# A recurrent layer and a gated feed-forward layer on one core: h transposed by VectorE and transfers instead of TensorE

## The chip, the core and the metric

The kernel runs on one core of a Trainium2 chip. A core has TensorE (PE in the profile; its weight loads are PEld), VectorE (DVE), ScalarE (ACT), GpSimd (POOL) and SyncE (SP), which here issues the data transfers. Each engine runs its own instructions in the order in which they were written, and waits on semaphores where it needs another's result. The metric is the device time of one execution in microseconds. Before the change the median of three runs is 543.51 us (543.43 to 544.18).

## What is computed

Two layers in a row, each with a layer norm before it and one behind it, and a residual sum. x is (2, 1024, 512), all in float32. Cut to what matters:

```python
def rnn(x, W_in, b_in, W_out, b_out, gamma, beta):        # hidden 1024
    u = einsum('bsd,hd->bsh', x, W_in) + b_in
    s_t = tanh(u_t + s_{t-1} * gamma + beta)              # 1024 steps in time
    return einsum('bsh,dh->bsd', s, W_out) + b_out

def ffn(x, gate_w, up_w, down_w, gate_scale, up_scale, down_scale):   # inner 1536
    q(x, w, scale) = (x @ w.astype(float8_e4m3fn).astype(float32)) * scale
    return q(silu(q(x, gate_w, gate_scale)) * q(x, up_w, up_scale), down_w, down_scale)

x = x + layernorm(rnn(layernorm(x), ...))
x = x + layernorm(ffn(layernorm(x), ...))
```

## The kernel before

The 1024 time steps of each of the two sequences are cut into 8 segments that run side by side, so a step works on 16 columns (2 sequences x 8 segments) of 1024 hidden values, a tile of 128x128. A segment is 128 steps, taken in 8 blocks of 16 steps; a block holds 16 x 16 = 256 tokens, which is two token tiles of 128 (numbers i = 2k and 2k + 1 of block k). The segments start from states that are warmed up over 96 steps first. All of it is one program, and the order of the work on every engine is written out by hand.

The first part (to about 168 us of the profile) loads and rounds the weights, computes u for all blocks, and runs the warm-up and the steps of blocks 0 and 1. The part that the change touches is the loop from L545 on. It goes over 8 blocks k of 12 slices fc, and one slice is one column of 128 of the inner 1536. In slice i:

- TensorE: `mm_g(i)` multiplies the gate and up weights with h of block k, 16 matmuls of 256 columns, h being given as two parts hT and hL (a rounded value and what the rounding left), then `down(i - 2)` adds two earlier results, each as the parts fH and fL, into the two token tiles of the block, 4 matmuls of 512 columns. `mm_g` uses three buffers in turn.
- ScalarE: `gate(i - 1)`, the Silu, then the rounded part fH.
- VectorE: `f_in(i - 1)` (f, L447), and `f_low(i - 1)` (fL, L455), which `down(i - 1)` needs in slice i + 1. Both come one slice behind `mm_g`.

Between these, the loop carries three other strands, in slices chosen by hand:

1. `main_step(k + 2, t)`, the recurrence of the block after the next: two instructions on VectorE (z, L260 and L261), a tanh on ScalarE (L262), each step waiting for the one before. `STEPS` says how many of a block's 16 steps stand in each slice: the first of the pair is for steps ahead of `f_low`, the second for steps behind it. `go(n)` writes up to n of them; `go(K)` all that are left of the slice. Blocks 6 and 7 have none.
2. What makes h of block k + 1, for its two token tiles: `mm_y` (output projection, 8 products of 512 columns in two passes each, L384), `y_in` (bias and statistics, L394 and L116), `y_resid` (residual sum onto the rows of x, and statistics, L401), `y_norm` (h, L409), `trans_h` (four transposes on TensorE into PSUM, L130) and `split_h` (hT by ScalarE, L423, hL by VectorE, L424). Statistics go on to GpSimd (`var`, `rstd`), which gives the reciprocal deviation; the row behind it on VectorE waits for that. The rows of x are loaded again by `load_r` (L376) at the end of slice 1, as their buffers (four in turn) come free: a load waits until `o_out` of block k - 1 has read the buffer. In block 0 there are no `mm_y` and no loads in the loop: the first four token tiles are projected and loaded ahead of it, and the first two (block 0's own) go through `trans_h` and `split_h` there.
3. What ends block k - 1: `o_in`, `o_stat`, `o_out` in slice 1, and two stores of 256 KB on SyncE ahead of the two loads. `check_piece` (L493, ScalarE, slices 3, 6, 9 and 11 of blocks 0 to 5) and `verdict` (slice 7 of block 6) check that the segmented result may be used; a fallback program follows that is not run here.

Before the change the slices of strand 2 are: `mm_y` in 1 and 4, `y_in` in 2 and 5, `y_resid` in 4 and 6, `y_norm` in 4 and 8, `trans_h` in 5 and 9, `split_h` in 6 and 10.

`us[0]` is the tile of block 0's states (8 KB of each partition); after the first two `mm_y`, and the first step of block 1, nothing reads it.

Of the kernel before, what the change touches and what calls it, by code (L numbers as in the profile page):

```python
# [9 lines left out]
F32 = mybir.dt.float32  # L10
# [4 lines left out]
ALU = mybir.AluOpType  # L15
# [3 lines left out]
P = 128  # L19
# [13 lines left out]
def segmented(  # L33
# [21 lines left out]
    nc = tc.nc  # L55
# [3 lines left out]
    ND, NH, NI = D // P, H // P, I // P  # L59
# [54 lines left out]
    def stats(src):  # L114
        st = small.tile([P, nc.vector.BN_STATS_DIM], F32, tag="st", name="st")
        nc.vector.bn_stats(st, src)  # L116
        return mean_rstd(st)
# [10 lines left out]
    def transposed(pt, src):  # L128
        for dc in range(ND):
            nc.tensor.transpose(pt[:, dc, :], src[:, dc * P : (dc + 1) * P], ident)  # L130

    us = {}
# [12 lines left out]
    held = {}  # L145
# [112 lines left out]
    def main_step(k, t):  # L258
        z = small.tile([P, NH, GB], F32, tag="z", name=f"z_{k}_{t}", bufs=2)
        nc.vector.tensor_tensor(z, coef, run["state"], ALU.mult)  # L260
        nc.vector.tensor_tensor(z, z, us[k][:, :, t], ALU.add)  # L261
        nc.scalar.activation(us[k][:, :, t], z, AF.Tanh)  # L262
        run["state"] = us[k][:, :, t]
# [67 lines left out]
    for n in range(NB - 1):  # L331
        mine = []
        for t in range(K):
# [26 lines left out]
            if n in (1, 2, 3, 4) and t == 9:  # L360
                c = slice((n - 1) * NH // 4, n * NH // 4)
# [17 lines left out]
    def mm_y(i, part=range(NH)):  # L379
        k, t0 = i // 2, (i % 2) * TT  # L380
        if part[0] == 0:
            held["py", i] = ps_y.tile([P, D], F32, tag="py", name=f"py_{i}")
        for hc in part:
            nc.tensor.matmul(  # L384
                held["py", i],
                lhsT=us[k][:, hc, t0 : t0 + TT, :].rearrange("p t q -> p (t q)"),
                rhs=wout_sb[:, hc, :],
                start=(hc == 0),
                stop=(hc == NH - 1),
            )  # L390

    def y_in(i):
        y = held["y", i] = yw.tile([P, D], F32, tag="y", name=f"y_{i}", bufs=1)
        nc.vector.tensor_tensor(y, held["py", i], bout_bc, ALU.add)  # L394
        held["ymr", i] = stats(y)

    def y_resid(i):

        m, r = held["ymr", i]
        x1 = held["x", i]  # L400
        nc.vector.scalar_tensor_tensor(x1, held["y", i], r, x1, ALU.mult, ALU.add)  # L401
        c = held["c", i] = small.tile([P, 1], F32, tag="c", name=f"c_{i}", bufs=8)
        nc.gpsimd.tensor_tensor(c, m, r, ALU.mult)
        held["xmr", i] = stats(x1)

    def y_norm(i):
        m, r = held["xmr", i]
        h = held["h", i] = yw.tile([P, D], F32, tag="h", name=f"h_{i}")
        nc.vector.tensor_scalar(h, held["x", i], m, r, ALU.subtract, ALU.mult)  # L409

    def trans_h(i):
        pool, tag = (ps_d, "pd") if i == 1 else (ps_t, "pt")
        pt = held["ph", i] = pool.tile([P, ND, P], F32, tag=tag, name=f"ph_{i}")
        transposed(pt, held["h", i])

    def split_h(i):

        k, j = i // 2, i % 2
        if j == 0:
            held["hT", k] = hw.tile([P, ND, N], F32R, tag="hT", name=f"hT_{k}")  # L420
            held["hL", k] = hw.tile([P, ND, N], F32R, tag="hL", name=f"hL_{k}")
        hT, hL = (held[a, k][:, :, j * P : (j + 1) * P] for a in ("hT", "hL"))
        nc.scalar.copy(hT, held["ph", i])  # L423
        nc.vector.tensor_tensor(hL, held["ph", i], hT.bitcast(F32), ALU.subtract)  # L424


    def mm_g(i):
        k, fc = divmod(i, NI)
        pg = held["g", i] = ps_g.tile([P, 2, N], F32, tag="pg", name=f"pg_{i}")
        for n, w in enumerate((gate_sb, up_sb)):  # L430
            for dc in range(ND):
                for part in ("hT", "hL"):
                    nc.tensor.matmul(  # L433
                        pg[:, n, :],
                        lhsT=w[:, dc, fc * P : (fc + 1) * P],
                        rhs=held[part, k][:, dc, :],
                        start=(dc == 0 and part == "hT"),
                        stop=(dc == ND - 1 and part == "hL"),
                    )

    def gate(i):
        g = held["gate", i] = fw.tile([P, N], F32, tag="gate", name=f"gate_{i}")
        nc.scalar.activation(g, held["g", i][:, 0, :], AF.Silu, scale=ffs[:, 0, i % NI : i % NI + 1])  # L443

    def f_in(i):
        f = held["f", i] = fw.tile([P, N], F32, tag="f", name=f"f_{i}")
        nc.vector.scalar_tensor_tensor(  # L447
            f, held["g", i][:, 1, :], ffs[:, 1, i % NI : i % NI + 1], held["gate", i], ALU.mult, ALU.mult
        )
        fH = held["fH", i] = fw.tile([P, N], F32R, tag="fH", name=f"fH_{i}")  # L450
        nc.scalar.copy(fH, f)  # L451

    def f_low(i):
        fL = held["fL", i] = fw.tile([P, N], F32R, tag="fL", name=f"fL_{i}")
        nc.vector.tensor_tensor(fL, held["f", i], held["fH", i].bitcast(F32), ALU.subtract)  # L455

    def down(i, j):
        k, fc = divmod(i, NI)
        if fc == 0:
            held["d", 2 * k + j] = ps_d.tile([P, D], F32, tag="pd", name=f"pd_{k}_{j}")  # L460
        for part in ("fH", "fL"):
            nc.tensor.matmul(  # L462
                held["d", 2 * k + j],
                lhsT=held[part, i][:, j * P : (j + 1) * P],
                rhs=down_sb[:, fc, :],
                start=(fc == 0 and part == "fH"),
                stop=(fc == NI - 1 and part == "fL"),
            )

    def o_in(i):  # L470
        o = held["o", i] = pool.tile([P, D], F32, tag="o", name=f"o_{i}", bufs=2)
        nc.vector.tensor_tensor(o, held["d", i], dsc_bc, ALU.mult)
# [49 lines left out]
    n = NB - 1  # L522
# [17 lines left out]
    mm_y(3, range(6, NH))  # L540


    STEPS = {0: (1, 0), 1: (1, 3), 3: (1, 1), 4: (0, 3), 7: (1, 0), 8: (0, 1), 9: (1, 0), 10: (0, 1), 11: (1, 1)}
    last = NB * NI - 1
    for i in range(last + 3):  # L545
        k, fc = divmod(i, NI)
        more = k + 1 < NB
        steps = iter(())
        if k + 2 < NB:
            t0 = sum(sum(STEPS.get(c, ())) for c in range(fc))  # L550
            before, after = STEPS.get(fc, (0, 0))
            steps = iter(range(t0, t0 + before + after))

        def go(n):
            for t in islice(steps, n):
                main_step(k + 2, t)

        if i <= last:
            mm_g(i)
        if i >= 2:  # L560
            for j in range(2):
                down(i - 2, j)
        if more:
            if fc == 1 and k:
                mm_y(2 * k + 2)
            if fc == 4 and k:
                mm_y(2 * k + 3)
            if fc in (5, 9):
                trans_h(2 * k + 2 + (fc - 5) // 4)
        live = 1 <= i <= last + 1  # L570
        if live:
            gate(i - 1)
            f_in(i - 1)

        if more and fc == 2:
            y_in(2 * k + 2)
        elif more and fc == 4:
            y_resid(2 * k + 2)
        elif more and fc == 5:
            y_in(2 * k + 3)  # L580
        elif more and fc in (6, 10):
            split_h(2 * k + 2 + (fc - 6) // 4)
        elif more and fc == 8:
            y_norm(2 * k + 3)
        else:
            go(1)
        if live:
            f_low(i - 1)
        ends = [2 * k - 2, 2 * k - 1] if k else []
        if fc == 1 and k:  # L590
            for j in ends:
                o_in(j)
            go(1)
        if k and fc == (1 if more or k == NB else 2):
            for j in ends:
                o_stat(j)
            go(1)
        for j in ends:
            if fc == (1 if more or k == NB else 3 + j % 2):
                o_out(j)  # L600
                go(1)
        if more and fc == 1 and k:
            for j in range(2):
                load_r(2 * k + 2 + j)
        if more and fc == 4:
            go(2)
            y_norm(2 * k + 2)
        if more and fc == 6:
            y_resid(2 * k + 3)
        go(K)  # L610
        if k + 2 < NB and fc in (3, 6, 9, 11):
            check_piece(4 * k + (3, 6, 9, 11).index(fc))
        if k + 2 == NB and fc == 7:
            verdict()
            others = [e for e in mybir.ALL_ENGINES if e != mybir.EngineType.PE]
            redo = nc.values_load(flag[0:1, 0:1], engines=others, min_val=0, max_val=2 * P)
# [384 lines left out]
```

## Time and profile before

| | |
|---|---|
| median of 3 runs | 543.51 us |
| the profiled execution | 543.2 us |
| its span, first to last instruction | 541.4 us |
| mean granted TensorE clock | 0.993 |
| blocks 1 to 5 of the loop | 48.0 us each |
| TensorE transposes of h (L130 ph) on the chain from 170 us on | 1.4% |

The page lists for each engine the busy time and its share of the span. The chain of waits is the work that ended last, followed back from the end; in the loop it is TensorE almost throughout. A timeline row has start, length, engine, line, operation, result and operands, and in brackets the idle time of the engine just before it with what ended it. PE rows overlap (a matmul's end is modelled), so PE's times here are taken from start to start.

### The profile page before, as it was taken

The page shows a single profiled execution, that of the slowest core. Times are in us where ns is not written, and L with a number is a line of the kernel's source. Part 1 is how long each engine was busy: PE and PEld are TensorE (multiplying, and loading weights), DVE is VectorE, ACT ScalarE, POOL GpSimd, SP SyncE. Part 2 cuts the span into 40 slices and gives each one's busy share as a digit, 9 for nine tenths or more (in the row PEclk, how much of TensorE's full clock was granted, in tenths as well). Part 3 has the DMA queues.
Part 4 walks back from the last instruction along what each step waited for, and adds up shares of the span by engine and source line. Part 5 has one row for each costly group of instructions (what it writes and reads, how often), then busy time and mean ns, then how long its engine had stood idle before and what let it go on. Part 6 is the DMA issues. An engine that isn't in the chain of part 4 may idle for free.

```text
span 541.4 us, 8064 instructions
## 1 busy us (share of the span) xinstructions
PE 515.2 (95%) x2818; PEld 408.6 (75%) x2818; DVE 360.3 (67%) x1017; ACT 225.4 (42%) x590; POOL 55.7 (10%) x152
## 2 busy tenths in 40 slices
PE   3999999999999899999999999999999999999991
PEld 2888877776547787789669777966987796689990
DVE  3488888886675767765856775585677657364634
ACT  1366666665423453335225333522533351123330
POOL 1111110010011111110110111010101101110101
PEclk9999999999999999999999999999999999999997
DMA  7653545332000000200200020011002001100101
GB/s 185 181 187 110 159 153 156 118 89 87 21 1 2 0 1 0 79 2 0 46 32 1 2 78 1 1 31 49 0 2 79 1 1 28 50 1 1 41 1 44
DMA packets 15808, 27.36 MB, mean 51 GB/s; under 512 B 1424, under 2 KB 3984, under 8 KB 15760
## 3 DMA queue, kind: packets, MB, share of 16 engines
q1 hardware_dynamic: 15344, 26.49, 16.7%
q8 instruction: 24, 0.39, 0.3%
q10 hardware_dynamic: 416, 0.27, 0.2%
q14 instruction: 24, 0.20, 0.1%
HBM read 22.57 MB, written 4.19 MB: 49 GB/s over the span
## 4 chain that ended last, share of the span: by engine, by line
PE 66%; DVE 19%; ACT 8%; issue 3%; DMA 1%; POOL 1%; ACTq 0%; DVEq 0%; POOLq 0%
PE pg L433 30%; PE py L384 17%; PE pd L462 15%; DVE zw L247 5%; ACT sw L249 5%; DVE zw L246 5%; PE pu L218 3%; DVE z L261 2%; DVE z L260 2%; ACT us L262 2%; PE ph L130 1%; DMA x<-in_x_dram 1%; DVE st L116 1%; DVE st L192 1%; DVE mv L121 1%
## 5 line engine op out<-in xcount | busy, mean ns | idle before, releaser
L218 PE MATMUL pu<-xT,win_sb 128*128 128x256 f32 x512 | 123.2, 391 | 2.3 <-ACT xT L211 0.5
L218 PEld LDWEIGHTS pu<-xT,win_sb 128*128 128x128 f32 x512 | 95.1, 193 | 26.3 <-ACT us L227 13.8
L384 PE MATMUL py<-wout_sb,us 128*128 128x512 f32 x256 | 112.4, 592 | 1.0 <-DVE y L394 1.0
L433 PE MATMUL pg<-hT,gate_sb 128*128 128x256 f32 x384 | 100.6, 297 | 0.0
L433 PE MATMUL pg<-hL,gate_sb 128*128 128x256 f32 x384 | 93.9, 280 | 0.0
L433 PE MATMUL pg<-hL,up_sb 128*128 128x256 f32 x384 | 93.3, 279 | 0.0
L433 PE MATMUL pg<-hT,up_sb 128*128 128x256 f32 x384 | 93.2, 278 | 0.0
L447 DVE SCALAR_TENSOR_TENSOR f<-pg,ffs,gate 128x256 f32<-128x256 f32 x96 | 46.1, 481 | 68.2 <-ACT gate L443 68.2
L384 PEld LDWEIGHTS py<-wout_sb,us 128*128 128x128 f32 x256 | 48.4, 190 | 56.4 <-issue 54.1
L262 ACT ACTIVATE us<-z 128x128 f32<-128x128 f32 x128 | 39.7, 310 | 101.4 <-DVE z L261 99.1
L462 PE MATMUL pd<-down_sb,fL 128*128 128x512 f32 x192 | 75.9, 395 | 1.9 <-DVE fL L455 1.8
L433 PEld LDWEIGHTS pg<-hT,gate_sb 128*128 128x128 f32 x384 | 72.4, 189 | 6.1 <-issue 3.1
L433 PEld LDWEIGHTS pg<-hL,gate_sb 128*128 128x128 f32 x384 | 72.3, 188 | 5.8 <-issue 2.9
L462 PE MATMUL pd<-down_sb,fH 128*128 128x512 f32 x192 | 76.1, 396 | 0.0
L451 ACT CAST fH<-f 128x256 fp32r<-128x256 f32 x96 | 39.0, 407 | 80.7 <-DVE f L447 80.1
L433 PEld LDWEIGHTS pg<-hT,up_sb 128*128 128x128 f32 x384 | 72.5, 189 | 0.0
L433 PEld LDWEIGHTS pg<-hL,up_sb 128*128 128x128 f32 x384 | 72.3, 188 | 0.0
L443 ACT ACTIVATE gate<-pg,ffs 128x256 f32<-128x256 f32 x96 | 44.9, 468 | 59.8 <-PE pg L433 55.5
L123 POOL TENSOR_SCALAR var<-mv 128x1 f32<-128x1 f32 x64 | 14.2, 223 | 471.1 <-DVE mv L121 470.3
L455 DVE TENSOR_TENSOR fL<-f,fH 128x256 fp32r<-128x256 f32 x96 | 40.2, 418 | 10.9 <-ACT fH L451 10.3
L260 DVE TENSOR_TENSOR z<-coef,us 128x128 f32<-128x128 f32 x127 | 36.3, 286 | 12.2 <-ACT us L262 12.0
L249 ACT ACTIVATE sw<-zw 128x120 f32<-128x120 f32 x95 | 28.8, 303 | 34.4 <-DVE zw L247 34.3
(69 smaller groups left out, 508.8 us busy)
## 6 DMA issues: line engine op xcount, KB each, us to landing
xr<-in_x_dram SPq DMA_DIRECT2D x16, 256.0 KB
out_dram<-o SPq DMA_DIRECT2D x16, 256.0 KB
x<-in_x_dram SPq DMA_DIRECT2D x14, 256.0 KB
ws<-in_gate_w_dram SPq DMA_DIRECT2D x12, 256.0 KB
ws<-in_up_w_dram SPq DMA_DIRECT2D x12, 256.0 KB
ws<-in_down_w_dram SPq DMA_DIRECT2D x12, 256.0 KB
win_sb<-in_w_in_dram SPq DMA_DIRECT2D x4, 512.0 KB
wout_sb<-in_w_out_dram SPq DMA_DIRECT2D x4, 512.0 KB
```

The lines of the kernel that those rows point to most:

```text
L218: nc.tensor.matmul(pu[:, 0, :], lhsT=win_sb[:, dc, hc * P : (hc + 1) * P], rhs=held["xT", n][:, dc, :], start=(dc == 0), stop=(dc == ND - 1),)
L246: nc.vector.tensor_tensor(z, coefw, run["state"], ALU.mult)
L249: nc.scalar.activation(s, z, AF.Tanh)
L260: nc.vector.tensor_tensor(z, coef, run["state"], ALU.mult)
L262: nc.scalar.activation(us[k][:, :, t], z, AF.Tanh)
L384: nc.tensor.matmul(held["py", i], lhsT=us[k][:, hc, t0 : t0 + TT, :].rearrange("p t q -> p (t q)"), rhs=wout_sb[:, hc, :], start=(hc == 0) ...
L433: nc.tensor.matmul(pg[:, n, :], lhsT=w[:, dc, fc * P : (fc + 1) * P], rhs=held[part, k][:, dc, :], start=(dc == 0 and part == "hT"), stop= ...
L443: nc.scalar.activation(g, held["g", i][:, 0, :], AF.Silu, scale=ffs[:, 0, i % NI : i % NI + 1])
L447: nc.vector.scalar_tensor_tensor(f, held["g", i][:, 1, :], ffs[:, 1, i % NI : i % NI + 1], held["gate", i], ALU.mult, ALU.mult)
L451: nc.scalar.copy(fH, f)
L455: nc.vector.tensor_tensor(fL, held["f", i], held["fH", i].bitcast(F32), ALU.subtract)
L462: nc.tensor.matmul(held["d", 2 * k + j], lhsT=held[part, i][:, j * P : (j + 1) * P], rhs=down_sb[:, fc, :], start=(fc == 0 and part == "fH ...
```

## The change

In all blocks but the first, h is transposed by VectorE, in squares of 32x32: `turn_h` writes the squares of one token tile into the first half of `us[0]`. When the second tile's squares are there, 16 transfers on SyncE's queue, of 32 partitions x 1 KB each, move the squares to their places in the second half of `us[0]`. `split_h` reads there, not in PSUM, for both tiles. `trans_h` stays for the first two tiles, ahead of the loop. In the loop the output projections stand in slices 1 and 2, `y_in` in 2 and 3, `y_resid` in 2 and 4, `y_norm` in 2 and 4, `turn_h` in 2 and 5, `split_h` in 9 and 10, and the 16 steps of the recurrence are dealt to the slices anew. The loads of the rows of x stay at the end of slice 1.

```diff
+    Q = 32
+
+    def turn_h(i):
+        j = i % 2
+        room = us[0].rearrange("p a b c -> p (a b c)").rearrange("p (m a c n) -> p m a c n", m=2, a=P // Q, c=ND)
+        squares, held["hr"] = room[:, 0], room[:, 1]
+        nc.vector.transpose(
+            squares[:, :, :, j * Q : (j + 1) * Q].rearrange("p a c n -> p c a n"),
+            held["h", i].rearrange("p (c a n) -> p c a n", c=ND, a=P // Q),
+        )
+        if j == 1:
+            for a in range(P // Q):
+                for t in range(P // Q):
+                    nc.sync.dma_start(
+                        out=held["hr"][a * Q : (a + 1) * Q, t], in_=squares[t * Q : (t + 1) * Q, a]
+                    )
...
     def split_h(i):
...
-        nc.scalar.copy(hT, held["ph", i])
-        nc.vector.tensor_tensor(hL, held["ph", i], hT.bitcast(F32), ALU.subtract)
+        if k == 0:
+            src = held["ph", i]
+        else:
+            hT, hL = (t.rearrange("p c (t n) -> p t c n", n=Q) for t in (hT, hL))
+            src = held["hr"][:, :, :, j * Q : (j + 1) * Q]
+        nc.scalar.copy(hT, src)
+        nc.vector.tensor_tensor(hL, src, hT.bitcast(F32), ALU.subtract)
...
-    STEPS = {0: (1, 0), 1: (1, 3), 3: (1, 1), 4: (0, 3), 7: (1, 0), 8: (0, 1), 9: (1, 0), 10: (0, 1), 11: (1, 1)}
+    STEPS = {0: (1, 0), 1: (1, 3), 2: (0, 4), 3: (0, 1), 4: (0, 1), 7: (1, 1), 8: (1, 1), 11: (1, 0)}
...
-            if fc == 4 and k:
+            if fc == 2 and k:
                 mm_y(2 * k + 3)
-            if fc in (5, 9):
-                trans_h(2 * k + 2 + (fc - 5) // 4)
...
-        if more and fc == 2:
-            y_in(2 * k + 2)
+        if more and fc in (2, 3):
+            y_in(2 * k + fc)
         elif more and fc == 4:
-            y_resid(2 * k + 2)
+            y_resid(2 * k + 3)
         elif more and fc == 5:
-            y_in(2 * k + 3)
-        elif more and fc in (6, 10):
-            split_h(2 * k + 2 + (fc - 6) // 4)
-        elif more and fc == 8:
-            y_norm(2 * k + 3)
+            turn_h(2 * k + 3)
+        elif more and fc in (9, 10):
+            split_h(2 * k + 2 + fc - 9)
         else:
             go(1)
         if live:
             f_low(i - 1)
...
-        if more and fc == 4:
+        if more and fc == 2:
+            y_resid(2 * k + 2)
             go(2)
             y_norm(2 * k + 2)
-        if more and fc == 6:
-            y_resid(2 * k + 3)
+            go(1)
+            turn_h(2 * k + 2)
+        if more and fc == 4:
+            y_norm(2 * k + 3)
         go(K)
```

## The prediction

> **What bounds the kernel now.** I read the busy shares first, then the chain of waits, then the timelines of one block. All times are us from the start of the profiled span of 541.4. The shares, and the stretch of one whole block (columns of the second line: stretch, then busy time and count on PE, PEld, DVE, ACT, POOL, clock, DMA share, GB/s):
>
> ```profile
> PE 515.2 (95%) x2818; PEld 408.6 (75%) x2818; DVE 360.3 (67%) x1017; ACT 225.4 (42%) x590; POOL 55.7 (10%) x152
> ...
> 351.00:399.00 48.00, 48.00 (x283) 38.21 (x282) 32.14 (x86) 19.12 (x50) 5.28 (x14) 1.00 0.08 23
> ```
>
> PE has no gap in a 48.0 us block, at full clock; DVE has 15.9 us of room per block. The chain (start, length, work) gives PE's prices:
>
> ```profile
> 370.25 6.87 PE py L384 x16
> 377.12 1.89 PE pg L433 x16
> 379.01 0.94 PE pd L462 x4
> 379.95 0.44 PE ph L130 x4
> ```
>
> A slice costs PE 1.86 (gate and up) + 0.92 (down) = 2.78; an output projection 6.87; four transposes 0.44. But a share says nothing of a block's inside. VectorE in block 3 (362.10 is y_in), and SyncE's loads of the residual rows:
>
> ```profile
> 362.10 0.68 DVE L394 TENSOR_TENSOR y<-py,bout_bc 128x512 f32<-128x512 f32 x1
> 362.81 0.69 DVE L116 BATCH_NORM_STATS2 st<-y 128x6 f32<-128x512 f32 x1
> 363.54 0.18 DVE L121 BATCH_NORM_AGGREGATE mv<-st 128x2 f32<-128x6 f32 x1
> 363.64 0.39 DVE L455 TENSOR_TENSOR fL<-f,fH 128x256 fp32r<-128x256 f32 x1
> ...
> 368.79 0.75 DVE L401 SCALAR_TENSOR_TENSOR xr<-y,rstd,xr 128x512 f32<-128x512 f32 x1 [0.36 <-DMA xr<-in_x_dram]
> ```
> ```profile
> 362.51 1.31 SPq L376 DMA_DIRECT2D xr<-in_x_dram  x2
> ```
>
> y_resid already waits for the load, two slices after y_in. It starts 6.69 after y_in here, 7.06, 6.96 and 6.33 in the other blocks where it waits, at most 5.98 and 6.42 where it doesn't. Last, block 0, which has no output projections, and there PE already waits for fL:
>
> ```profile
> 178.73 0.50 PE L462 MATMUL pd<-down_sb,fL 128*128 128x512 f32 x1 [0.92 <-DVE fL L455]
> ```
> ```profile
> 180.63 0.31 ACT L262 ACTIVATE us<-z 128x128 f32<-128x128 f32 x1 [0.68 <-DVE z L261]
> 180.84 0.83 ACT L493 ACTIVATE junk<-gate_sb 128x768 fp8e4<-128x768 f32 x1
> ...
> 181.67 0.46 ACT L443 ACTIVATE gate<-pg,ffs 128x256 f32<-128x256 f32 x1
> ...
> 187.12 0.31 ACT L262 ACTIVATE us<-z 128x128 f32<-128x128 f32 x1 [0.69 <-DVE z L261]
> 187.34 0.46 ACT L443 ACTIVATE gate<-pg,ffs 128x256 f32<-128x256 f32 x1
> ```
>
> So ScalarE runs a slice's Silu only behind the tanh of every step that stands before it. From these rows and VectorE's beside them: step to step 0.99; a step's first multiply to its tanh 0.64; tanh to the next slice's f 0.71, or 1.53 with a check piece between; f to fL 1.95 with y_in between, 2.00 with y_resid; y_resid 1.61; statistics to the row that needs the rstd 1.13 (162.30 to 163.43); fL to PE's second down matmul 0.44.
>
> **Removed.** 56 transposes in 14 groups: 14 x 0.44 = 6.2 off PE, 0.88 per block. The page "TensorE: Matmul & The Clock Gate" (Part 4: PE-mode transpose) of the Trainium skill gives about 275 ns for one in a kernel's context; this trace shows 0.44 / 4 = 0.11, and the row decides. By the page 56 x 0.275 = 15.4 would go, and the sum below would be 553.
>
> **Added on VectorE.** 14 transposes of 128x512. The trace has none. Nearest rows at the same width: h, 0.46 to the next instruction, as the lower end; statistics, 0.73, and y, 0.72; twice such a pass, 1.4, as the upper end. I take 0.72, one pass. The page "VectorE: DVE Perf Modes" (The three transpose paths) gives 311 ns for 128x128 in bf16, and says that it yields 32x32 blocks only. An estimate from it is 4 x 0.311 = 1.24; no row here shows it, and it would add 0.52 x 2 x 6 = 6 to the sum.
>
> **Added on SyncE.** 112 transfers of 32 KB, 16 per block, issued when the second transpose is done; in that queue only stores and loads of slice 1 stand before them. One issue takes between 0.33 and 0.60 in the rows:
>
> ```profile
> 58.23 0.33 SPq L169 DMA_DIRECT2D ws<-in_up_w_dram  x1
> ```
> ```profile
> 28.48 0.60 SPq L154 DMA_DIRECT2D x<-in_x_dram  x1
> ```
>
> These are two-dimensional like the first, so 0.33 and 0.06 between: 16 x 0.39 = 6.2, then about 2.0 to land (the last wait for a store at the end of the span is 2.0). I come back to the end 0.66. split_h now reads SBUF in runs of 32; its rows (hT 0.58, hL 0.69) are kept, since at 256 columns f from PSUM (0.48) and fL from SBUF (0.42) cost nearly the same; twice their length would still fit the 1.5 spared below.
>
> **Moved.** The projections stay in PE's sum. In slices 2 to 5 the order on VectorE is now y_resid, two steps, y_norm, a step, turn_h, a step; then f(2), y_in, fL(2), a step; f(3), y_resid, fL(3), y_norm, a step; f(4), turn_h, fL(4). Behind y_resid's wait, which now comes at once, all of that is queued, and PE waits for fL.
>
> *Block 3, replayed.* PE without waits: slice 2 from 361.94, projection to 371.55, slice 3 to 374.33, gate/up of slice 4 to 376.19; fL(2), fL(3), fL(4) are used at 376.42, 379.20, 381.98. VectorE: y_resid 368.79; steps at 370.40 and 371.39; h 371.92; step 372.38; turn_h 372.91 to 373.63; step 373.63, tanh 374.27; f(2) 374.98; fL(2) 376.93, used 377.37: 0.95 late. Step 377.24, tanh 377.88, check piece, f(3) 379.41; fL(3) 381.41, used 381.85, 2.65 late. Its y_resid's statistics at 381.31 let h start at 382.44; step 382.90, tanh 383.54, f(4) 384.25; turn_h 384.65 to 385.37; fL(4) 385.37, used 385.81, **3.8 late in all**. From slice 6 on, with fewer steps, VectorE catches up and nothing waits. Less the 0.88: +2.9 per block. The five loads' mean delay (at most 6.62) is close to this block's 6.69, so 5 x 2.9 = +14.5.
>
> *The transfers.* Issued from 385.5, landed by 393.7. ScalarE comes to split_h at about 394.3, and PE needs fL(8) at 396.96; from landing to it is 0.1 + two copies of 0.61 + 0.44 = 1.75. So a landing up to 395.2 is hidden: 1.5 to spare. Cover: slices 6 to 9.
>
> *Block 0.* Rows are loaded, so y_resid starts with its rstd: 178.19 + 1.13 = 179.32. Steps 180.93, 181.92; h 182.45; step 182.91; turn_h 183.44 to 184.16; step 184.16, tanh 184.80; f(2) 185.51; fL(2) 187.46, used 187.90, where PE is ready at 181.59: 6.3 of waiting, as no projection covers the slice. On: f(3) 189.94, fL(3) 191.94, used 192.38, PE's down(3) ends 193.1 and gate/up 195.06; h 192.97, step 193.43, f(4) 194.78, turn_h 195.18, fL(4) 195.90, used 196.35; down(4) ends 197.05. Before it ended at 191.04, waits of its own included. +6.0 - 0.44 for the second group = +5.6.
>
> *Block 6* has no steps: the load's wait (464.35) fits, turn_h ends 468.3, fL(2) by 470.6, needed at 472.4. It gains 0.88, and the wait before the check's tiny matmul, 481.81 to 482.39, should go, since y_resid has left slice 6: -1.5.
>
> **Sum.** 541.4 + 5.6 + 14.5 - 1.5 = 560.0 of span. The profiled execution took 543.2, 1.8 more than its span; the median 543.51 is 0.3 above it. So 543.5 + 18.6 = **562.1**. Transpose at 0.46 and loads at 6.0: 1.2 less per block of 1 to 5, 0.5 less in block 0, 555.5. Transpose at 1.4: 1.36 more in each of six, 570.3.
>
> **Rivals.**
> 1. *The transfers come late* (slower still). At 0.66 an issue they land at 385.5 + 10.6 + 2.0 = 398.1, 2.9 after the limit; six such blocks and 0.5 in block 6: 562 + 18 = 580. For: the stores' and x loads' rows. Against: the plain rows at 0.33. Issues of 0.5 would cost 2.
> 2. *The rows are there in time* (not slower). Place: y_resid in slice 2 of blocks 1 to 5. If the load lands by 364.95, within 2.4 us of its issue, the 3.8 vanishes and each of them gains 0.88: 543.5 + 5.6 - 4.4 - 1.5 = 543.2. Against: it took 6.3 and more wherever it was waited for, and it stands behind two stores that I see nothing move.
> 3. *PE's work alone counts* (faster): VectorE's lateness is absorbed also in block 0. The 6.2 go and block 6's 0.6: 543.5 - 6.8 = 536.7. For: DVE is 67% busy. Against: PE already waits for fL in block 0 with fewer steps ahead.
> 4. *A small loss*: block 0's alone and part of the others', 545 to 551.
>
> **Chances.** Forecast 0.75, rival 1 0.10, rival 2 0.05, rival 3 0.06, rival 4 0.04. What a measurement here can tell from no change is 0.2%, 1.1 us. Faster: rival 3 and a little of 2, 0.08; same: most of 2 and some of 4, 0.05; slower 0.87. The range holds the forecast's bounds, cut below at 550 and drawn up to 576 for the lesser half of rival 1.
>
> **What would show it.** Right: PE waiting for DVE fL about 3.8 us per block in slices 4 to 6; DVE L401 waiting for the load some 3 to 4 us in each of blocks 1 to 5; a first wait near 6 us in block 0; PE without ph outside the first block. The transposes' row tells 0.72 from its ends, SyncE's rows 0.39. Wrong: blocks of 47.1 us, or ScalarE's hT waiting for the transfers, or L401 without a wait.

## The result, and the profile after

The changed kernel takes 581.92 us (median of 4 runs, 579.8 to 582.45), the kernel before 543.47 beside it: the ratio is 1.0707 [1.0689, 1.0724]. The forecast was 562.1 with a range of 550 to 576, so the direction was right, the size was not, and the time lies above the range. The profiled run took 579.8, with a span of 578.0, 36.6 more than before.

The page of the changed kernel: the shares, the clock in 40 slices, and the chain that ended last by engine.

```profile
PE 521.8 (90%) x2762; PEld 407.4 (70%) x2762; DVE 368.4 (64%) x1031; ACT 223.5 (39%) x590; POOL 54.9 (9%) x152
...
PEclk9999999999998899998999999899999999999997
...
DVE 34%; PE 28%; ACT 11%; SPq 9%; DMA 8%; issue 6%; POOL 2%; ACTq 1%; DVEq 0%; POOLq 0%
```

The 56 transposes are gone from PE (2818 matmuls before, 2762 now), and yet its busy time rose from 515.2 to 521.8. Part of the rise is the clock, which dips in the middle of the span, so that the same matmuls take longer there; as the end of a matmul is modelled, the sum is no measure of what was lost. PE falls from 95% to 90%. In the chain PE falls from 66% to 28%, and VectorE (34%), SyncE's queue (SPq, 9%) and the transfers (DMA, 8%) stand in its place. The idle time of PE, VectorE and ScalarE by what ended it, from 168 us on (total, number of waits, longest):

```profile
PE pd L486 <- DVE fL L479: 22.3, 18, 2.4
...
PE pd L486 <- ACT fH L475: 10.6, 12, 5.0
```
```profile
DVE xr L401 <- DMA xr<-in_x_dram: 28.8, 6, 5.1
```
```profile
ACT hT L447 <- DMA us<-us: 18.7, 7, 3.4
```

VectorE's y_resid (L401) waits for the rows of x, and ScalarE's hT for the 16 transfers. Neither wait hurts by itself; PE waits for f's two parts, which are queued behind these.

Where the 36.6 went is read from the starts of `y_in` of a block's first token tile (L394), one in each block:

| us | before | forecast | after | without the transfers (e2) | e8 |
|---|---|---|---|---|---|
| block 0's y_in to block 1's | 42.29 | 47.9 | 49.44 | 46.99 | 42.27 |
| the five blocks behind it, mean | 47.80 | 50.7 | 54.10 | 51.39 | 47.11 |
| block 6's y_in to the end | 83.38 | 81.9 | 82.06 | 82.04 | 81.99 |

The steps behind it are 7.15 in block 0, 31.5 in the five blocks, and -1.3 from block 6 on; the loop's first y_in is 0.7 earlier.

One block shows both losses. It is the block that the prediction replays (k = 4 counted from 0; the prediction calls it block 3). VectorE, and PE's waits in slices 4 to 6 (a row has start, length, work, and in brackets the idle time before it):

```profile
389.65 0.68 DVE L394 TENSOR_TENSOR y<-py,bout_bc 128x512 f32<-128x512 f32 x1
...
396.45 0.75 DVE L401 SCALAR_TENSOR_TENSOR xr<-y,rstd,xr 128x512 f32<-128x512 f32 x1 [4.86 <-DMA xr<-in_x_dram]
...
400.56 0.70 DVE L424 STREAM_TRANSPOSE us<-h 128x512 f32<-128x512 f32 x1
401.18 0.25 DVE L260 TENSOR_TENSOR z<-coef,us 128x128 f32<-128x128 f32 x1
...
404.44 0.39 DVE L479 TENSOR_TENSOR fL<-f,fH 128x256 fp32r<-128x256 f32 x1
```
```profile
404.89 0.50 PE L486 MATMUL pd<-down_sb,fL 128*128 128x512 f32 x1 [0.87 <-DVE fL L479]
...
407.96 0.50 PE L486 MATMUL pd<-down_sb,fH 128*128 128x512 f32 x1 [0.28 <-ACT fH L475]
409.39 0.50 PE L486 MATMUL pd<-down_sb,fL 128*128 128x512 f32 x1 [0.93 <-DVE fL L479]
...
412.91 0.51 PE L486 MATMUL pd<-down_sb,fH 128*128 128x512 f32 x1 [0.72 <-ACT fH L475]
...
426.66 0.50 PE L486 MATMUL pd<-down_sb,fL 128*128 128x512 f32 x1 [1.88 <-DVE fL L479]
```

The rows of x arrive 6.80 after y_in and everything behind y_resid on VectorE shifts with them, so fL(2) ends when PE has long wanted it. By the starts of PE's gate products, slices 4, 5 and 6 take 3.93, 4.50 and 3.98 instead of 2.78 each: 4.07 lost. Slices 7 to 9 lose nothing. Then slice 10 takes 4.95, 2.17 lost, and the rows of SyncE, ScalarE and VectorE say why:

```profile
413.04 10.10 SPq L431 DMA_DIRECT2D us<-us  x16
```
```profile
424.92 0.62 ACT L447 CAST hT<-us 128x512 fp32r<-128x512 f32 x1 [2.96 <-DMA us<-us]
```
```profile
425.57 0.69 DVE L448 TENSOR_TENSOR hL<-us,hT 128x512 fp32r<-128x512 f32 x1 [4.11 <-ACT hT L447]
426.18 0.42 DVE L479 TENSOR_TENSOR fL<-f,fH 128x256 fp32r<-128x256 f32 x1
```

The 16 issues fill 10.10 us of the queue, the last lands 1.8 later, and only then can hT, hL and, queued behind hL, the fL that PE needs be made. Such a wait of PE stands in each of blocks 0 to 5 (2.18, 2.05, 2.45, 1.92, 1.88, 1.41). Block 0's other loss is the wait that the prediction looked for, in two pieces:

```profile
185.76 0.79 PE L486 MATMUL pd<-down_sb,fH 128*128 128x512 f32 x1 [4.96 <-ACT fH L475]
...
187.13 0.79 PE L486 MATMUL pd<-down_sb,fL 128*128 128x512 f32 x1 [0.58 <-DVE fL L479]
```

The matmuls behind these waits take 0.79 instead of 0.50; this is a dip of the clock. The stretches in which it shows (stretch, length, busy time and count on PE, PEld, DVE, ACT, POOL, clock, DMA share, GB/s):

```profile
184.00:191.00 7.00, 4.66 (x16) 3.86 (x17) 4.57 (x10) 2.98 (x8) 1.02 (x3) 0.52 0.00 0
262.80:266.20 3.40, 3.36 (x12) 3.07 (x13) 2.17 (x6) 1.62 (x5) 0.00 (x0) 0.50 0.00 0
372.00:376.00 4.00, 4.00 (x20) 3.70 (x20) 2.70 (x7) 2.32 (x6) 0.00 (x0) 0.57 0.01 2
```

### The profile page after: what moved, and what is told of

Read it like the earlier page. It is cut to its first block, busy times and chain, and to the rows that moved or that the text cites. A ratio compares the mean times of both kernels' runs of the same rounds, so it can differ in the third digit from the quotient of the medians.

```text
span 578.0 us, 8147 instructions
## 1 busy us (share of the span) xinstructions
PE 521.8 (90%) x2762; PEld 407.4 (70%) x2762; DVE 368.4 (64%) x1031; ACT 223.5 (39%) x590; POOL 54.9 (9%) x152
## 4 chain that ended last, share of the span: by engine, by line
DVE 34%; PE 28%; ACT 11%; SPq 9%; DMA 8%; issue 6%; POOL 2%; ACTq 1%; DVEq 0%; POOLq 0%
PE pg L457 14%; SPq L431 9%; PE pd L486 8%; DMA xr<-in_x_dram 6%; DVE zw L247 5%; ACT sw L249 5%; DVE zw L246 5%; DVE z L261 4%; DVE st L116 4%; DVE z L260 4%; PE py L384 4%; PE pu L218 3%; ACT us L262 2%; ACT gate L467 2%; DMA us<-us 2%
## 5 line engine op out<-in xcount | busy, mean ns | idle before, releaser
L486 PE MATMUL pd<-down_sb,fL 128*128 128x512 f32 x192 | 79.5, 414 | 22.3 <-DVE fL L479 22.3
L457 PE MATMUL pg<-hL,gate_sb 128*128 128x256 f32 x384 | 95.6, 283 | 0.0
L486 PE MATMUL pd<-down_sb,fH 128*128 128x512 f32 x192 | 78.6, 410 | 10.7 <-ACT fH L475 10.6
L457 PEld LDWEIGHTS pg<-hT,gate_sb 128*128 128x128 f32 x384 | 74.0, 193 | 6.9 <-issue 3.1
L457 PEld LDWEIGHTS pg<-hL,gate_sb 128*128 128x128 f32 x384 | 74.0, 193 | 6.6 <-issue 2.9
L486 PEld LDWEIGHTS pd<-down_sb,fL 128*128 128x128 f32 x192 | 36.8, 192 | 34.6 <-DVE fL L479 30.1
L467 ACT ACTIVATE gate<-pg,ffs 128x256 f32<-128x256 f32 x96 | 44.4, 463 | 24.1 <-PE pg L457 20.4
L486 PEld LDWEIGHTS pd<-down_sb,fH 128*128 128x128 f32 x192 | 36.5, 190 | 16.7 <-ACT fH L475 13.9
```

The source lines that it names most:

```text
L457: nc.tensor.matmul(pg[:, n, :], lhsT=w[:, dc, fc * P : (fc + 1) * P], rhs=held[part, k][:, dc, :], start=(dc == 0 and part == "hT"), stop= ...
L486: nc.tensor.matmul(held["d", 2 * k + j], lhsT=held[part, i][:, j * P : (j + 1) * P], rhs=down_sb[:, fc, :], start=(fc == 0 and part == "fH ...
```

## The experiments

Two causes were proposed for the blocks behind block 0, the late rows of x (slices 4 to 6) and the late transfers (slice 10), beside block 0's own packed steps. All edits are against the changed kernel. Ratios are to the kernel before, run on the same chip; 1% is 5.4 us.

**e1: the splits one slice later.** This gives the transfers one slice of 2.78 more.

```diff
-        elif more and fc in (9, 10):
-            split_h(2 * k + 2 + fc - 9)
+        elif more and fc in (10, 11):
+            split_h(2 * k + 2 + fc - 10)
```

> The changed kernel with split_h in slices 10 and 11, not 9 and 10. Theory A (the 16 issues of 0.63 us each make the transfers land some 2.7 us after TensorE's need in slice 10, in blocks 0 to 5): one slice of 2.78 us more covers it, the wait for fL in slice 10 goes, 6 x 2.7 = 16 and about 2.5 of lost clock behind the two longest waits: 563 to 567 us. Theory B (the time goes to VectorE's added work, the transposes and the steps packed into slices 1 to 4, and the wait for the transfers only shows it): 578 to 582 us.

Measured: 570.61, ratio 1.0524 [1.0503, 1.0546], 3.6 us above the upper end of 563 to 567. The waits in slice 10 are gone, but the second split now ends too late for the next block's first products. PE's new waits, in the blocks' first slices:

```profile
PE pg L457 <- DVE hL L448: 1.6, 5, 0.3
...
PE pg L457 <- ACT hT L447: 1.2, 3, 0.4
```

So the transfers' lateness has two possible victims, the fL of slice 10 or the start of the next block, and one slice of delay trades part of the one for the other. The run supports the cause; its size needed the next run.

**e2: no transfers.** The squares are used where VectorE leaves them. Left out is the movement of the squares to their places.

```diff
-        if j == 1:
-            for a in range(P // Q):
-                for t in range(P // Q):
-                    nc.sync.dma_start(
-                        out=held["hr"][a * Q : (a + 1) * Q, t], in_=squares[t * Q : (t + 1) * Q, a]
-                    )
+        held["hr"] = squares
```

> The changed kernel without the 112 transfers: split_h reads the squares where VectorE wrote them, so h is left with its squares out of place and the output is not the reference's. Theory A: the wait in slice 10 goes, as in the run with split_h later: 563 to 567 us. Theory B: 578 to 582 us. If the transfers also held up other loads and stores of the queue, it comes out lower than the run with split_h later.

Measured: 563.18, ratio 1.0377 [1.0357, 1.0398]: a hit. The transfers cost 0.033 of 543, 17.9 us, and no wait in slice 10 is left. What remains is the time that was forecast for the whole change, and the waits that it rests on are unchanged: VectorE's for the rows of x sum to 29.9, where they were 28.8.

**e3: the rows of x earlier.** A fifth buffer for the rows, with h's two buffers cut to one for space; the first tile's load moves to the end of slice 11 of the block before.

```diff
-    xr = late.enter_context(tc.tile_pool(name="xr", bufs=4))
+    xr = late.enter_context(tc.tile_pool(name="xr", bufs=5))
...
-        h = held["h", i] = yw.tile([P, D], F32, tag="h", name=f"h_{i}")
+        h = held["h", i] = yw.tile([P, D], F32, tag="h", name=f"h_{i}", bufs=1)
...
-            for j in range(2):
-                load_r(2 * k + 2 + j)
+            load_r(2 * k + 3)
+        if k + 2 < NB and fc == 11:
+            load_r(2 * k + 4)
```

> The changed kernel with the first of a block's two loads of rows of x issued at the end of slice 11 of the block before (five buffers for these rows, one for h). Theory C (y_resid's wait of about 5 us for the load in slice 2 is what makes fL late in slices 4 to 6 of blocks 1 to 5): the 4.3 us there go, 5 x 4.3 = 21, while the transfers still land about 2.2 late: 558 to 563 us. Theory B (fL is late there because more steps, y_in, y_resid and a transpose stand ahead of it): over 574 us.

Measured: 564.26, ratio 1.0395 [1.0375, 1.0415], 1.3 above the upper end of 558 to 563. In the loop y_resid waits for no load any more, and all of PE's waits in slices 4 to 6 of the blocks behind block 0 are gone; the waits in slice 10 stay, up to 2.60. The clock is 0.972 in the profiled run and 0.972 to 0.978 in the four, against 0.981 in the changed kernel, so more was lost behind the waits that stayed. The late rows cost 1.0707 - 1.0395, or 17.0 us.

**e4: e3 and e1 together.** No further edit.

> Both edits. Theories A and C together leave block 0's loss (5.6 us and about 1.4 of lost clock), take 0.88 off each of blocks 1 to 5 and 1.5 off block 6: 543 to 546 us, not measurably other than the kernel before. Theory B: over 565 us.

Measured: 549.56, ratio 1.0125 [1.0106, 1.0144], 3.6 us above the upper end of 543 to 546. PE's waits from 168 us on:

```profile
PE pd L486 <- ACT fH L475: 5.3, 2, 5.0
PE pg L457 <- DVE hL L448: 1.6, 5, 0.3
PE pd L486 <- DVE fL L479: 1.5, 2, 0.9
PE pg L457 <- ACT hT L447: 1.2, 3, 0.4
```

The pd waits are block 0's alone (5.0 of the 5.3 for fH is one wait). The pg waits are e1's new ones at the block starts, to the tenth: making the rows early did not make the transfers early enough. Seen from e1, the early rows are worth 1.0524 - 1.0125, or 21.7 us.

**e5: block 0 in the old order.** Block 0 alone gets the old slices, the old steps and TensorE's transposes; its core:

```diff
+    STEPS0 = {0: (1, 0), 1: (1, 3), 3: (1, 1), 4: (0, 3), 7: (1, 0), 8: (0, 1), 9: (1, 0), 10: (0, 1), 11: (1, 1)}
...
+            S_ = STEPS if k else STEPS0
...
+            if fc in (5, 9) and k == 0:
+                trans_h(2 * k + 2 + (fc - 5) // 4)
```

> The changed kernel with block 0 alone as before: its strands and steps in the old slices, its h by TensorE. Theory D (in block 0 eight steps and the y work stand ahead of fL with no output projection to cover them, and the long wait halves TensorE's clock for 7 us): its loss of some 7 us against the kernel before goes, 573 to 576 us. Theory E (the lateness is passed on, block 1 then waits as much longer): 579 to 582 us.

Measured: 573.36, ratio 1.0577 [1.0555, 1.0599]: within the 573 to 576 of the theory that block 0's loss is its own (D). The 7.1 us gained are the 7.15 by which block 0 had grown, and the later blocks keep their losses.

**e6: the same transfers from two queues.** Every third issue goes to GpSimd's queue, 5 of the 16. This tells the issuing (A1) from the moving of the data (A2).

```diff
-                    nc.sync.dma_start(
+                    queue = nc.gpsimd if (4 * a + t) % 3 == 2 else nc.sync
+                    queue.dma_start(
```

> The changed kernel with 5 of a block's 16 transfers issued by GpSimd, 11 by SyncE; nothing else. Theory A1 (what is late is the issuing, 0.63 us each in one queue): SyncE is done 3.2 us earlier, the landing is within TensorE's need in slice 10, 563 to 568 us. Theory A2 (what is late is the moving of the data, or the semaphores that the transfers share): 577 to 582 us. If GpSimd's issues hold up the rstd behind them, more.

Measured: 563.02, ratio 1.0365 [1.0349, 1.0382], the time of e2, which moves nothing. GpSimd's five issues and ScalarE's wait behind them in one block of e6:

```profile
350.07 2.52 POOL L432 DMA_DIRECT2D us<-us  x5 [3.52 <-ACT gate L468]
```
```profile
358.81 0.62 ACT L448 CAST hT<-us 128x512 fp32r<-128x512 f32 x1 [0.33 <-DMA us<-us]
```

hT waits at most 0.33 in e6, where it waited up to 3.42 before. The same bytes move; what was late was the issuing in one queue. A second queue could also have moved the data faster, but there was little to gain by that: in the changed kernel the last transfer landed 1.8 after the last issue. The Trainium skill, "DMA: Bandwidth & Descriptors" (Rules for kernel authors), says that spreading transfers over several issuing engines brings no bandwidth and "only saves sequencer issue time". This run agrees: the issue time was the whole of the 1.0707 - 1.0365, or 18.6 us.

**e7: everything mended at once.** e4 and e5, and the second `turn_h` moved from slice 5 to the end of slice 4, right behind its `y_norm`, so that its transfers start earlier.

```diff
-        elif more and fc == 5:
-            turn_h(2 * k + 3)
...
         if more and k and fc == 4:
             y_norm(2 * k + 3)
+            turn_h(2 * k + 3)
```

> Rows early, split_h in slices 10 and 11, block 0 as before, and the second turn_h of a block at the end of slice 4 right behind y_norm. If theories A, C and D name all the losses, blocks 1 to 5 run at 48.0 - 0.88 = 47.1 us, block 6 is 1.5 shorter, block 0 as before: 542.2 - 5.9 = 536.3, 535 to 539 us, faster than the kernel before. If something of the change's cost is still unnamed: 542 us or more.

Measured: 543.07, ratio 1.0007 [0.9997, 1.0017], where 535 to 539 was expected. The blocks took 47.83 to 48.45, with one wait of PE in each. VectorE, ScalarE and PE there:

```profile
284.32 0.71 DVE L424 STREAM_TRANSPOSE us<-h 128x512 f32<-128x512 f32 x1
284.95 0.25 DVE L260 TENSOR_TENSOR z<-coef,us 128x128 f32<-128x128 f32 x1
...
286.27 0.48 DVE L471 SCALAR_TENSOR_TENSOR f<-pg,ffs,gate 128x256 f32<-128x256 f32 x1 [0.74 <-ACT gate L467]
```
```profile
285.56 0.31 ACT L262 ACTIVATE us<-z 128x128 f32<-128x128 f32 x1 [3.98 <-DVE z L261]
285.78 0.46 ACT L467 ACTIVATE gate<-pg,ffs 128x256 f32<-128x256 f32 x1
...
286.84 0.40 ACT L475 CAST fH<-f 128x256 fp32r<-128x256 f32 x1 [0.61 <-DVE f L471]
```
```profile
287.30 0.49 PE L486 MATMUL pd<-down_sb,fH 128*128 128x512 f32 x1 [0.57 <-ACT fH L475]
```

The transpose now stands ahead of the step of slice 4. That step's tanh stands ahead of the Silu (L467) on ScalarE, which idles 3.98 for it, and f, fH and PE follow. PE's wait is 0.57, and its next products come 1.06 late.

**e8: that step one slice later.** Against e7:

```diff
-    STEPS = {0: (1, 0), 1: (1, 3), 2: (0, 4), 3: (0, 1), 4: (0, 1), 7: (1, 1), 8: (1, 1), 11: (1, 0)}
+    STEPS = {0: (1, 0), 1: (1, 3), 2: (0, 4), 3: (0, 1), 5: (1, 0), 7: (1, 1), 8: (1, 1), 11: (1, 0)}
```

> The kernel of the run before with one step moved from the end of slice 4 to slice 5, so that f(4) follows turn_h at once and its Silu does not stand behind that step's tanh. There down(4) waited 0.57 for fH, and TensorE's next products came 1.06 late, in each of blocks 1 to 5 (a little more in block 1). Theory F (this one wait is all that is left): 543.1 - 5.5 = 537 to 539 us, faster than the kernel before. Theory G (a lateness that goes round among the slices, VectorE being too full for 47.1 us): 541 to 544 us.

Measured: 538.39 (537.12 to 539.61) against 542.61, ratio 0.9914 [0.9899, 0.9928]: within the expected 537 to 539, and faster than both kernels. PE's waits from 168 us on, and 48 us from the middle of the loop:

```profile
PE pd L486 <- DVE fL L479: 1.8, 2, 0.9
PE ph L130 <- DVE h L409: 1.0, 1, 1.0
PE pg L457 <- DVE hL L448: 0.3, 1, 0.3
```
```profile
303.00:351.00 48.00, 48.00 (x280) 38.28 (x280) 33.36 (x86) 19.48 (x53) 5.06 (x14) 1.00 0.12 34
```

PE has no gap at full clock, as in the kernel before, but a block takes 47.11 instead of 47.80 by the table above, since PE's work is the same but for the transposes. One wait of 0.32, at the start of a block, is all that is left of the loop behind block 0.

## Why the prediction missed

**The step that failed** is in the part on SyncE: "These are two-dimensional like the first, so 0.33 and 0.06 between: 16 x 0.39 = 6.2". Two rows had been shown, a plain load of weights at 0.33 and a load of x at 0.60, and the nearer was chosen by the shape of the access. The issues of the changed kernel on SyncE (shortest/median/longest in ns):

```profile
L431 SPq DMA_DIRECT2D us<-us x112: 540/589/1405, 195.3 to 522.5; - x112
```

The median is 0.589, and 16 fill 10.1 to 10.9 us with the gaps between them: 0.63 to 0.68 each. The rest of that step held in the replayed block. The first issue came 23.39 after y_in where 385.5 - 362.10 = 23.4 was forecast. The landing took 1.8 where 2.0 was taken. With 10.10 for 6.2, hT began 35.27 after y_in, 3.67 behind the forecast landing. The prediction found 1.5 to spare, and PE came 0.27 later than forecast (4.07 lost before, not 3.8), which leaves 1.90; PE's wait there is 1.88. So the cover and the order were right, and one price was wrong. Over the kernel it cost 17.9 us (e2) to 18.6 (e6), of the 19.8 between 562.1 and the result. Not all of that is waiting: by the starts of the gate products, slices 10 and 11 of the six blocks took 16.6 more than in e2's trace, of which the six waits are 11.9 and two dips of the clock some 3.3 (below); the rest isn't resolved.

**Rival 1 came true.** It priced an issue at 0.66, lateness at 2.9 per block, and the time at 580, against 581.92. It was given 0.10. The trace before spoke, if anything, for the dearer price: the loads of the rows took 0.60 to 0.63 (16 issues) and the stores of the loop 0.63 to 0.70 (14), and 0.33 stood only in loads of weights ahead of the loop. The prediction says itself that a price between them, 0.5, would already cost 2 us. So 0.10 was far too little, and a range cut at 576 left out the case that came. That rival 1 also comes so near in time is partly luck: the waits were 1.41 to 2.45 per block and not 2.9, and the dips of the clock, which it did not have, made up for a good part of the difference.

**The rest of the sum.** For the kernel without late transfers the forecast of 562.1 stands against 563.18 (e2) and 563.02 (e6). Its terms hold less exactly than the sum, and the nearness is partly luck:

- The transpose on VectorE: 0.72 taken, 0.70 long and 0.62 to the next row measured. The estimate of 1.24 from the Trainium skill, "VectorE: DVE Perf Modes" (The three transpose paths), was too high; the nearest row of the trace was the better guide.
- The transposes on TensorE: the prediction set 0.11 against about 0.275 as if the two disagreed. In the trace before, one such matmul is 0.272 long (L130 ph, median of 64), and four take 0.44 from start to start. The length was never the price, and the prediction's 0.88 per block stands.
- The rows of x: y_resid was to wait 3 to 4 us and start 6.69 after y_in; it waited 4.84 to 5.14 in blocks 1 to 5 and started 6.80 after it in the replayed block. The loss there was to be 3.8 and was 4.07, with 0.95, 2.65 and 3.8 forecast behind the three slices and 1.15, 2.87 and 4.07 measured. In e2 five blocks grew by 17.98 (51.39 - 47.80 each) instead of 14.5.
- Block 0: +5.6 forecast, +4.70 in e2. Its first waits were 4.96 + 0.58 instead of 6.3. Behind them the clock is halved for 6.83 us, from 184 to 191, in e2 as in the changed kernel. PE was busy for 4.76 of these, so by an estimate half of that, 2.4, is the clock, which no term held; without it the term would have been some 3 too high, about what the five blocks' term was too low. In the changed kernel block 0 grew by 7.15, with the transfers' 2.18 added.
- Block 6: -1.5 forecast, -1.32 measured.
- Shown in their places, if not all in their size: L401's waits, fL and fH late in slices 4 to 6, no ph on PE behind the first block, and blocks of 47.1 (47.80 less PE's 0.88 is 46.9) once nothing is late (e8). Of the prediction's signs of being wrong, ScalarE's hT waiting for the transfers came with the first trace.

The clock was in no term. What a dip costs can be read inside the changed kernel's trace: slices 10 and 11 took 5.46 + 3.91 = 9.37 in block 3 (counted from 0), with a wait of 1.92 and a dip of 3.4 us, and 4.95 + 2.75 = 7.70 in block 4, with a wait of 1.88 and no dip, so the dip cost about 1.6. The four runs of e3, one kernel, point the same way: clocks of 0.972, 0.975, 0.977 and 0.978 went with 566.25, 564.74, 563.78 and 563.4. How much the clock cost over the whole kernel is not isolated by any run.

Rivals 2 and 3 fell with the first trace, since y_resid waits in each of blocks 1 to 5 and PE waits in block 0, and rival 4 with the time. Rival 3's 536.7 is nevertheless near what the idea is worth when nothing comes late: e8 takes 538.39, with block 0's two groups of transposes left that rival 3 had removed. It gets there by other slices and earlier loads, not because VectorE's lateness is absorbed. What was not tried is the new order with the rows early and TensorE's transposes kept; so how e8's gain divides between the transposes and the order is not measured by itself, only its agreement with PE's 0.88 per block.

## What to carry to other kernels

The time that a transfer takes its queue to issue did not shrink with its size here (medians of 0.59 for 32 KB, and of 0.33, 0.64 and 0.67 for 256 KB), so a strand cut into 16 transfers is priced by their number, and where two rows give two prices for an issue, the dearer one belongs in the range at full weight. A strand that is moved earlier has to bring along what it waits for: here the rows of x were loaded in time for the old place only, and an engine that works in order passed the wait on to everything queued behind it. What stands ahead of a short instruction on each engine, such as one tanh ahead of a Silu, can decide whether a change gains: e7 and e8 differ by one such step, and their ratios are 1.0007 and 0.9914.

## What the hardware showed that was not expected

The price of an issue does not follow its size: 32 KB between places of the on-chip memory took 0.63 to 0.68 of SyncE's queue, the 256 KB rows of x 0.66 (1.31 and 1.35 for two), and plain weight loads of 256 KB 0.33. What sets it between 0.33 and 0.66 is not shown. GpSimd's issues took 0.50 each (2.52 for five).

The granted clock halved behind some short waits of PE and not behind others. With waits of 4.96, 2.05 and 1.92 it was 0.50 from 184.27 to 191.10, from 262.77 to 266.18 and from 372.00 to 375.42; behind waits of 2.45, 2.18 and 1.88 it stayed at 1.00. The Trainium skill, "TensorE: Matmul & The Clock Gate" (HAM oscillation), gives a rule of no gap above some 3.4 us. The wait of 4.96 agrees with it. The rows of 2.05 and 1.92 go against it as a sufficient rule, since the clock fell behind shorter gaps. The dips of this trace last 3.41 us or twice that, and begin 78.50 and 109.23 apart, 23 and 32 times 3.413. So it may be the share of a fixed stretch of 3.41 us in which PE stands that counts, and not the length of a wait: in the stretches just before the three dips PE was busy for 0.00, 1.43 and 1.49 us, in those that held most of the waits of 1.88 and 2.45 for 1.58 and 1.76. This is not shown: in e5 the dip from 239.22 follows a stretch with 1.85, and no dip follows the stretch from 307.50, with 1.55. What decides among gaps of about 2 us stays open.
